# First edges of a graph layer: seven gather buffers of four chunks in place of three of eight, and a bfloat16 list of destinations

## The chip, the cores and the metric

The kernel runs on one core of one Trainium2 chip. The metric is the device time of one execution in microseconds; the time given is the median of several executions. A profile is one further execution, recorded by the hardware profiler: its span runs from the first to the last instruction, and its own time lies a little above the span.

## What is computed

One layer of a graph transformer over 6250 nodes of 256 features: a graph attention over 200000 edges sorted by destination, a linear attention over all nodes beside it, and then a mixture of four experts whose gate is itself a graph attention over 131072 edges.

```python
def reference(x, src, dst, W, a_src, a_dst, Wqkv, Wout, gamma, ...):
    xn = layernorm(x)
    # first edges
    z = einsum('ni,hid->nhd', xn, W)                  # 4 heads of 64
    es, ed = einsum('nhd,hd->nh', z, a_src), einsum('nhd,hd->nh', z, a_dst)
    e = leaky_relu(es[src] + ed[dst], 0.01)
    alpha = segment_softmax(e, dst)
    gnn = segment_sum(alpha * z[src], dst)
    x = x + gnn + linear_attention(xn, Wqkv, Wout, gamma)
    # second edges: a gate from a graph attention, top 2 of 4 experts
    return x + mixture_of_experts(layernorm(x), edge_index, ...)
```

## The kernel before

**Stages.** The kernel first normalizes the rows and projects them; for each node it stores a row of 264 floats, `z` with a one behind each head (260) and the four source terms, in the table `ztab` in DRAM. From the sorted edges it makes two lists on chip: `src_c`, for each edge the row of `ztab` to fetch, and `dl_c`, the destination's place within its tile of 128 nodes. Both are laid out with the edges of a chunk over the 128 partitions and one column per chunk; each tile of nodes has room for 33 chunks (28 for the last), 1612 chunks in all. Then comes the stage of the first edges, then that of the second edges with the experts.

**The first edges** (class `FirstEdges`, lines 762 to 854; its loop, 1018 to 1096). Chunks are taken in groups of `G1` = 8, 202 groups, the last of 4 chunks. For a group:

- `gather` (772, 774): one indirect DMA per chunk on POOL's queue fetches 128 rows of `ztab` into the group's tile `gt`, of 8 chunks. The pool `g1_g` has three such tiles.
- `sources` (786, with the helper at 208 to 210): VectorE subtracts the largest source term from the four terms of each gathered row (`L208`, into `src_d`), and ScalarE makes two exponentials of it (`src_f`).
- `load` (792): the destinations of the group's edges, spread to all partitions, are loaded on SP's queue as `br`; `one_hot_t` (807) compares them with the partition's number; `terms` (813) fetches the destination factors with matmuls against that one-hot matrix, and `terms_sum` (821) adds their three parts.
- `weights` (825, 827): each edge's weight, put into `dv`, a tile in PSUM that also holds the lane numbers.
- `weigh` (833): VectorE multiplies the gathered rows in place by the weights, four chunks at a time.
- `one_hot` (798): VectorE compares the lane numbers in `dv` with `dl_c`; the result `oh` is a float32 matrix per chunk.
- `add` (842): TensorE multiplies `oh` with the weighted rows, which sums them by destination; at a tile's end the sums are divided and stored (758 to 760, 849 to 851).

**What sets the order.** The loop writes the order out by hand. In turn g it begins with the gathers of group g+2 and the load of g+3, then does `weights`, `weigh` of chunks 0 to 3, `add` of those, `weigh` and `add` of chunks 4 to 7, with `terms`, `one_hot` and `sources` of group g+1 between and behind them. Between these stand small steps of the linear attention and the second norm (`mix_steps`; its row loads are line 978 and its joins with the sums 980 to 989), and the sort of the second edges. The framework tracks which instruction last used a piece of memory and adds the waits; it also moves instructions within an engine by its own estimate of their times, so the order on an engine is near that of the program but not always the same. A gather into a `gt` tile waits until the adds that read the tile's former content are done; POOL runs its queue in order, so what stands behind such a gather waits too.

**Ahead of and behind the stage.** A mask `before` (77) is made at the start and used only in `order_edges` (304, 305), a branch for edges that are not sorted. The lists are turned into columns by transposes and copied out of PSUM at 713. At the end of the stage the second norm writes its table `htab` (180, 181); the second edges gather from it at 1303, in groups of eight as well, 784 gathers; they write their one-hot matrix at 1324 and the messages at 1377. Their three short loads of the gate's norm are line 1268, the memsets of `first_of` are 1681 and 1683.

Of the kernel before, what the change touches and what calls it, by code (L numbers as in the profile page):

```python
# [9 lines left out]
F32 = mybir.dt.float32  # L10
BF16 = mybir.dt.bfloat16
I32 = mybir.dt.int32
U16 = mybir.dt.uint16
AF = mybir.ActivationFunctionType
OP = mybir.AluOpType
# [5 lines left out]
P = 128  # L21
# [4 lines left out]
EPS = 1e-5  # L26

G1 = 8
K1, K1L = 33, 28

ZW = 4 * 65
ZF = ZW + 4
# [29 lines left out]
def gps_layer(ctx: ExitStack, tc: tile.TileContext, a: dict, out: bass.AP):  # L62
# [9 lines left out]
    jp = cw.tile([P, P], I32, name="jp")  # L72
    G.iota(jp, pattern=[[1, P]], base=0, channel_multiplier=-1)
    ident = const.tile([P, P], F32, name="ident")
    V.tensor_scalar(ident, jp, 0.0, None, op0=OP.is_equal)
    before = const.tile([P, P], F32, name="before")
    V.tensor_scalar(before, jp, 0.0, None, op0=OP.is_gt)
    lane_i = cw.tile([P, P], I32, name="lane_i")
    G.iota(lane_i, pattern=[[1, P]], base=0, channel_multiplier=0)
    lane = const.tile([P, P], F32, name="lane")  # L80
# [119 lines left out]
    def source_factors(src_f, d, es, m2, slope):  # L200

        V.tensor_sub(d, es, m2[:, None, :].to_broadcast(list(es.shape)))  # L208
        S.activation(src_f[:, :, 0:4], d, AF.Exp, bias=shift_c)  # L209
        S.activation(src_f[:, :, 4:8], d, AF.Exp, scale=slope)  # L210

# [37 lines left out]
    S1 = len(chunk_tile)  # L249
    BS = (S1 + P - 1) // P  # L250
    src_c = ek.tile([P, BS * P], I32, name="src_c")
    dl_c = ek.tile([P, BS * P], F32, name="dl_c")
    over = ek.tile([1, 1], I32, name="over")
    start_k = ek.tile([P, 1], F32, name="start_k")
    first_t = ek.tile([P, B1], F32, name="first_t")
# [5 lines left out]
    def order_edges(w, bs, bd):  # L261

        C = (E1 + P - 1) // P
        room = kx.rearrange("p t d -> p (t d)")
        used = 0

        def take(n, dt, words):
            nonlocal used
            used += words
            assert used <= NT * D  # L270
            return room[:, used - words : used].bitcast(dt)[:, :n]

        o1, o2 = take(C, I32, C), take(C, I32, C)
        rec_ = take(2 * B1 * P, I32, 2 * B1 * P)
        R, rem = divmod(E1, C)
        pairs = dram.tile([B1 * P * P, 2], I32, name="pairs")
        src_i = o1
        dst_i = o2
        if rem:
            V.memset(src_i[96:P, rem:C], 0)  # L280
            V.memset(dst_i[96:P, rem:C], NT * P)
        for t_, d_ in ((src_i, a["src"]), (dst_i, a["dst"])):
            SP.dma_start(t_[:R], d_[0 : R * C].rearrange("(p c) -> p c", c=C))
            if rem:
                SP.dma_start(t_[R : R + 1, :rem], d_[R * C : E1].rearrange("(p c) -> p c", p=1))
        rec = rec_[:, : 2 * C].rearrange("p (c o) -> p c o", o=2)
        V.tensor_copy(rec[:, :, 0], src_i)
        V.tensor_copy(rec[:, :, 1], dst_i)
        addr = take(C, I32, C)
        V.tensor_single_scalar(addr, dst_i, 7, op=OP.arith_shift_right)  # L290
        tid = take(C, F32, C)
        V.tensor_scalar(tid, addr, float(NT), None, op0=OP.min)
        cnt = w.tile([P, NB], F32, name="cnt")
        hit = take(C, BF16, (C + 1) // 2)
        for b in range(NB):
            V.tensor_scalar(hit, tid, float(b), None, op0=OP.is_equal, op1=OP.add, accum_out=cnt[:, b : b + 1])
        off = w.tile([P, NB], F32, name="off")
        with tc.tile_pool(name="ord_p", bufs=1, space=PSUM) as ps:
            tot_p = ps.tile([NB, 1], F32, name="tot_p")
            T.matmul(tot_p, cnt, ones[:, 0:1], start=True, stop=True)  # L300
            tot = w.tile([NB, 1], F32, name="tot")
            V.tensor_copy(tot, tot_p)
            off_p = ps.tile([P, NB], F32, name="off_p")
            T.matmul(off_p, before, cnt, start=True, stop=False)
            T.matmul(off_p, tot[:, 0:1].to_broadcast([NB, P]), before[:NB, :NB], start=False, stop=True)
            V.tensor_copy(off, off_p)
        pos = o1.bitcast(F32)
        mask = take(C, U16, (C + 1) // 2)
        run = o2.bitcast(F32)
        for b in range(NB):  # L310
            V.tensor_scalar(mask, tid, float(b), None, op0=OP.is_equal)
            V.tensor_tensor_scan(run, mask, mask, off[:, b : b + 1], OP.add, OP.max)
            V.copy_predicated(pos, mask, run)
        V.tensor_scalar(addr, pos, 1.0, None, op0=OP.subtract)
        for c in range(C):
            i = G.indirect_dma_start(
                out=pairs[:, :],
                out_offset=bass.IndirectOffsetOnAxis(ap=addr[:, c : c + 1], axis=0),
                in_=rec[:, c, :],
                in_offset=None,  # L320
            )
            tc.declare_no_dep(i.ins, group="pairs", reason="each edge has a place of its own")
            tc.add_to_no_dep_group("pairs", i.ins)

        both = rec_.rearrange("p (b j o) -> p b j o", b=B1, o=2)
        V.tensor_copy(both[:, :, :, 0], bs)
        V.tensor_copy(both[:, :, :, 1], bd)
        full, r = divmod(E1, P * P)
        r, rest = divmod(r, P)
        if full:  # L330
            SP.dma_start(both[:, :full], pairs[0 : full * P * P].rearrange("(b r j) o -> r b j o", r=P, j=P))
        at = full * P * P
        if r:
            SP.dma_start(both[:r, full], pairs[at : at + r * P].rearrange("(r j) o -> r j o", j=P))
        if rest:
            at += r * P
            SP.dma_start(both[r : r + 1, full, :rest], pairs[at : at + rest].rearrange("(r j) o -> r j o", r=1))
        V.tensor_copy(bs, both[:, :, :, 0])
        V.tensor_copy(bd, both[:, :, :, 1])
# [422 lines left out]
    class FirstEdges:  # L762
# [6 lines left out]
            self.idx, self.dl, self.n, self.tiles = idx, dl, n, tiles  # L769

        def gather(self):
            self.gt = self.gp.tile([P, G1, ZF], F32, name="gt")
            for c in range(self.n):
                G.indirect_dma_start(  # L774
                    out=self.gt[:, c, :],
                    out_offset=None,
                    in_=ztab[:, :],
                    in_offset=bass.IndirectOffsetOnAxis(ap=self.idx[:, c : c + 1], axis=0),
                )

        def sources(self):

            n = self.n
            d = self.w.tile([P, G1, 4], F32, name="src_d", bufs=1)
            self.sf = self.w.tile([P, G1, 8], F32, name="src_f")
            source_factors(self.sf[:, :n], d[:, :n], self.gt[:, :n, ZW:], most_1, 0.01)

        def load(self, rows_):

# [31 lines left out]
            V.tensor_reduce(self.pw[:, :n], self.ed[:, :n].rearrange("p c (s f) -> p c f s", s=3), AX.X, OP.add)  # L821

        def weights(self):
            n, pw, gt = self.n, self.pw, self.gt
            V.tensor_mul(pw[:, :n], pw[:, :n], self.sf[:, :n])
            self.wp = self.dv[:, P : P + 4 * G1].rearrange("p (c h) -> p c h", h=4)
            V.tensor_max(self.wp[:, :n], pw[:, :n, 0:4], pw[:, :n, 4:8])

        def weigh(self, c0, c1):
            if c0 < self.n:  # L830
                c1 = min(c1, self.n)
                gz = self.gt[:, c0:c1, 0:ZW].rearrange("p c (h d) -> p c h d", h=4)
                V.tensor_mul(gz, gz, self.wp[:, c0:c1].unsqueeze(3).to_broadcast([P, c1 - c0, 4, 65]))  # L833

        def add(self, sums, s0, c0, c1):

            for c in range(c0, min(c1, self.n)):
                t = self.tiles[c]
                if t not in sums:
                    sums[t] = self.ps.tile([P, ZW], F32, name="ag")  # L840
                last = s0 + c + 1 == S1 or chunk_tile[s0 + c + 1] != t
                T.matmul(  # L842
                    sums[t], self.oh[:, c], self.gt[:, c, 0:ZW], start=(s0 + c == 0 or chunk_tile[s0 + c - 1] != t),
                    stop=last,
                )
                if last:
                    a3 = sums[t].rearrange("p (h d) -> p h d", h=4)
                    if t in joined:
                        z = self.w.tile([P, D], F32, name="z", bufs=1)
                        node_sums(self.w, a3[:, :, 0:64], a3[:, :, 64], z)  # L850
                        V.tensor_add(kx[: rows(t), t], kx[: rows(t), t], z[: rows(t)])
                    else:
                        node_sums(self.w, a3[:, :, 0:64], a3[:, :, 64], kx[:, t])
                    summed.add(t)
# [160 lines left out]

    n_hops = 2 * NT + 8 + 3 * NT + 10 + 6 * NT + 2 * NT + 26 + 5 * NT + 39

    with tc.tile_pool(name="g1_w", bufs=2) as w, tc.tile_pool(name="g1_g", bufs=3) as gp, tc.tile_pool(
        name="m_w", bufs=2
    ) as mxw, tc.tile_pool(name="m_k", bufs=1) as mxk, tc.tile_pool(name="g1_p", bufs=2, space=PSUM) as ps:  # L1020
        steps = mix_steps(mxw, mxk, ps)
# [76 lines left out]
    with tc.If(many != 0):  # L1098
# [7 lines left out]
        with tc.tile_pool(name="sl_k", bufs=1) as k, tc.tile_pool(name="sl_w", bufs=1) as w, tc.tile_pool(  # L1106
# [42 lines left out]
            with tc.For_i(0, NI, 1) as i:  # L1149
# [29 lines left out]
                grp.weights()  # L1179
                grp.weigh(0, 1)  # L1180
                ag = ps.tile([P, ZW], F32, name="ag")
                T.matmul(ag, grp.oh[:, 0], grp.gt[:, 0, 0:ZW], start=True, stop=True)
                a3 = ag.rearrange("p (h d) -> p h d", h=4)
                at = kx[:, ds(t, 1), :].rearrange("p a (h d) -> p (a h) d", h=4)
                V.tensor_add(at, at, a3[:, :, 0:64])
# [569 lines left out]
```

## Time and profile before

| | us |
|---|---|
| median of 3 runs | 3260.65 (3256.18 to 3268.05) |
| the profiled execution | 3258.8 |
| its span | 3257.0 |
| first gather of the first edges starts | 114.90 |
| last gather of the first edges ends | 2176.53 |
| first gather of the second edges starts | 2200.41 |
| last gather of the second edges ends | 3203.63 |

| engine | busy us | share of the span |
|---|---|---|
| DVE (VectorE) | 2439.4 | 75% |
| POOL (GpSimd) | 2344.4 | 72% |
| PE (TensorE) matmul | 2334.0 | 72% |
| PE weight load | 1699.4 | 52% |
| ACT (ScalarE) | 480.6 | 15% |

A line of a group of instructions reads: line of the kernel, engine, operation, written tile <- read tiles, number of instructions | busy time in us and mean ns of one | time for which the engine sat idle before them, and what ended most of that. In a timeline, a line reads: start and duration in us, engine, line, operation, tiles, and in brackets the engine's idle time before it and what ended it; "issue" is time in which the engine waited for nothing that the profile shows. Shares of busy time are means over stages that have different limits, so the stages are looked at one by one.

### The profile page before, as it was taken

The numbers are of one execution on the slowest core, as the hardware profiler recorded it, in microseconds if no ns is written. First come the engines' busy times: TensorE is split into PE (matmuls) and PEld (weight loads), VectorE is DVE, ScalarE is ACT, GpSimd is POOL, SyncE is SP. The second block draws the span as 40 slices with busy tenths as digits, with TensorE's granted clock in tenths as the row PEclk, the third lists the DMA queues.
The fourth block names the chain that finished last, engine by engine and source line by source line (L and its number), as shares of the span: only waits on it lengthen the run. The fifth ranks groups of instructions, "written<-read, shape, count | busy, mean of one in ns | idle before, by whom it ended". The sixth has DMA issues, their size and how long they took to land. (4 is left out here: it accounts for less than half of the span.)

```text
span 3257.0 us, 36396 instructions
## 1 busy us (share of the span) xinstructions
PE 2334.0 (72%) x10899; PEld 1699.4 (52%) x10900; DVE 2439.4 (75%) x6337; ACT 480.6 (15%) x1266; POOL 2344.4 (72%) x2436
## 2 busy tenths in 40 slices
PE   7677778865666574665665666658777877888888
PEld 5555666654455453554544545445455545555555
DVE  7587767788888887886886878667676766777775
ACT  3200111111111111111111111013111111111111
POOL 2577777777777777777777777757777777777772
PEclk9788888987888887787888878779998998999989
DMA  6544444445555555555555555534223223333321
GB/s 202 155 135 135 136 129 127 137 134 145 150 139 151 143 137 140 138 141 143 141 153 142 147 140 142 138 92 101 61 62 78 60 57 92 81 76 80 78 51 37
DMA packets 248273, 384.90 MB, mean 118 GB/s; under 512 B 73414, under 2 KB 156246, under 8 KB 248057
## 3 DMA queue, kind: packets, MB, share of 16 engines
q0 software_dynamic: 103296, 230.96, 28.9%
q1 hardware_dynamic: 142857, 150.87, 15.4%
q8 instruction: 91, 1.49, 0.2%
q14 instruction: 125, 1.02, 0.1%
q10 hardware_dynamic: 1904, 0.56, 0.1%
HBM read 345.44 MB, written 36.74 MB: 117 GB/s over the span
## 5 line engine op out<-in xcount | busy, mean ns | idle before, releaser
L774 POOL DMA_INDIRECT gt<-ztab,src_c x1612 | 1551.2, 962 | 528.1 <-issue 424.7
L842 PE MATMUL ag<-gt,oh 128*128 128x260 f32 x3224 | 980.1, 461 | 348.3 <-DVE gt L833 347.0
L842 PEld LDWEIGHTS ag<-gt,oh 128*128 128x128 f32 x3224 | 732.6, 234 | 516.0 <-DVE gt L833 375.9
L1303 POOL DMA_INDIRECT gt<-htab,src x784 | 764.6, 975 | 262.5 <-issue 210.0
L833 DVE TENSOR_TENSOR gt<-gt,dv 128x1040 f32<-128x1040 f32 x403 | 488.8, 1223 | 0.2 <-DVE src L409 0.2
L1424 PE MATMUL yo<-w,hT 128*128 128x256 f32 x1568 | 420.8, 411 | 15.8 <-DVE ys L1467 15.8
L1404 PE MATMUL hp<-xy,w 128*128 128x512 f32 (+1 forms) x832 | 407.2, 612 | 8.6 <-ACT hT L1409 4.5
L1424 PEld LDWEIGHTS yo<-w,hT 128*128 128x128 f32 x1568 | 303.5, 203 | 96.1 <-issue 26.3
L208 DVE TENSOR_TENSOR src_d<-gt,most 128x32 f32<-128x32 f32 x204 | 38.6, 189 | 355.6 <-DMA gt<-ztab,src_c 344.3
L868 PE MATMUL m<-wqkv,xy 128*128 128x256 f32 (+1 forms) x784 | 235.8, 436 | 88.8 <-DVE kmax L879 43.6
L798 DVE TENSOR_TENSOR oh<-dv,dl_c 128x1024 f32<-128x1024 f32 x202 | 243.9, 1207 | 0.0
L868 PEld LDWEIGHTS m<-wqkv,xy 128*128 128x128 f32 (+1 forms) x784 | 160.7, 215 | 125.1 <-DVE kmax L879 49.6
L1404 PEld LDWEIGHTS hp<-xy,w 128*128 128x128 f32 x832 | 159.9, 205 | 112.4 <-issue 98.3
L1409 ACT ACTIVATE hT<-hp,b 128x512 f32<-128x512 f32 (+1 forms) x208 | 132.8, 660 | 517.6 <-PE hp L1404 294.9
L209 ACT ACTIVATE src_f<-src_d,shift_c 128x32 f32<-128x32 f32 x202 | 64.9, 321 | 928.2 <-DVE src_d L208 836.3
L1361 DVE TENSOR_TENSOR pr<-dv,gt 128x64 f32<-128x64 f32 x98 | 21.9, 223 | 227.0 <-DMA gt<-htab,src 219.5
L1385 PE MATMUL ag<-mq,oh 128*128 128x120 bf16 x784 | 66.3, 236 | 150.4 <-DVE mq L1377 141.0
L813 PE MATMUL ed<-pw,ohT 128*128 128x24 bf16 x1612 | 72.1, 175 | 125.5 <-DVE ohT L807 111.1
L373 DVE MAX8 src<-dl 128x8 f32<-128x1024 f32 x128 | 156.0, 1219 | 0.4 <-issue 0.4
L1385 PEld LDWEIGHTS <-oh 128*128 128x128 bf16 x784 | 51.6, 107 | 198.5 <-DVE mq L1377 176.6
L375 DVE MATCH_REPLACE8 dl<-src,dl 128x1024 f32<-128x1024 f32 x127 | 153.4, 1208 | 0.0
L813 PEld LDWEIGHTS <-ohT 128*128 128x128 bf16 x1612 | 64.0, 98 | 165.4 <-DVE ohT L807 134.3
(350 smaller groups left out, 2695.0 us busy)
## 6 DMA issues: line engine op xcount, KB each, us to landing
br<-rows SPq DMA_DIRECT2D x299, 256.0 KB
gt<-ztab,src_c POOLq DMA_INDIRECT x1612
gt<-htab,src POOLq DMA_INDIRECT x784
early<-ys SPq DMA_DIRECT2D x24, 512.0 KB
ys<-early SPq DMA_DIRECT2D x24, 512.0 KB
ztab<-zt SPq DMA_DIRECT2D x48, 132.0 KB
row<-in_x_dram SPq DMA_DIRECT2D x48, 128.0 KB
out_dram<-ys SPq DMA_DIRECT2D x48, 128.0 KB
```

Of the source, the lines that this page charges most:

```text
L373: V.max(out=srtf[:, 8 * i : 8 * i + 8], in_=keyf)
L375: V.match_replace(out=keyf, in_to_replace=srtf[:, 8 * i : 8 * i + 8], in_values=keyf, imm_value=0.0)
L774: G.indirect_dma_start(out=self.gt[:, c, :], out_offset=None, in_=ztab[:, :], in_offset=bass.IndirectOffsetOnAxis(ap=self.idx[:, c : c + 1 ...
L798: V.tensor_tensor(self.oh[:, :n], self.dv[:, None, :P].to_broadcast([P, n, P]), self.dl[:, :, None].to_broadcast([P, n, P]), op=OP.is_equal,)
L813: T.matmul(self.ed[:, c, :], self.ohT[:, c * P : (c + 1) * P], pw3[:, ds(self.tiles[c], 1), :].rearrange("p a b -> p (a b)"), start=True, ...
L833: V.tensor_mul(gz, gz, self.wp[:, c0:c1].unsqueeze(3).to_broadcast([P, c1 - c0, 4, 65]))
L842: T.matmul(sums[t], self.oh[:, c], self.gt[:, c, 0:ZW], start=(s0 + c == 0 or chunk_tile[s0 + c - 1] != t), stop=last,)
L868: T.matmul(out_, xy[:, t, j, :n], wqkv[:, j, c0 : c0 + D], start=(j == 0), stop=(j == 1))
L1303: G.indirect_dma_start(out=self.gt[:, c, : tab.shape[1]], out_offset=None, in_=tab[:, :], in_offset=bass.IndirectOffsetOnAxis(ap=self.idx[ ...
L1404: T.matmul(hp[:, :m], wts[e][0][:, c, j * P : (j + 1) * P], xy[:, t0 : t0 + nt, c] if m == nt * P else xy[:, t0, c, :m], start=(c == 0), s ...
L1409: S.activation(h[:, :m], hp[:, :m], AF.Gelu, bias=b1[:, e, j : j + 1])
L1424: T.matmul(yo[:n], hT[j][:, o : o + n], wts[e][1][:, j, :], start=(j == 0 and e < EARLY), stop=(j == 3))
```

## The change

The tile of a group's gathered rows is split: `gather` takes a new tile of `GH` = 4 chunks from the pool at chunks 0 and 4, and the pool has seven such tiles, room for 28 chunks in place of 24. The functions that read `gt` take the tile and the chunk within it. `sources` makes its subtraction once per tile of four, and one pair of exponentials for the group as before (the helper `source_factors` is cut in two for it). The list `dl_c` is held as bfloat16, in half the memory; it holds whole numbers within a tile. The mask `before` is now made in the branch that uses it.

```diff
@@
 G1 = 8
+GH = 4
@@
-    before = const.tile([P, P], F32, name="before")
-    V.tensor_scalar(before, jp, 0.0, None, op0=OP.is_gt)
@@
         V.tensor_sub(d, es, m2[:, None, :].to_broadcast(list(es.shape)))
+        factors_of(src_f, d, slope)
+
+    def factors_of(src_f, d, slope):
         S.activation(src_f[:, :, 0:4], d, AF.Exp, bias=shift_c)
         S.activation(src_f[:, :, 4:8], d, AF.Exp, scale=slope)
@@
-    dl_c = ek.tile([P, BS * P], F32, name="dl_c")
+    dl_c = ek.tile([P, BS * P], BF16, name="dl_c")
@@ in order_edges
+        jp_ = w.tile([P, P], I32, name="jp_")
+        G.iota(jp_, pattern=[[1, P]], base=0, channel_multiplier=-1)
+        before = w.tile([P, P], F32, name="before")
+        V.tensor_scalar(before, jp_, 0.0, None, op0=OP.is_gt)
@@ FirstEdges.gather
-            self.gt = self.gp.tile([P, G1, ZF], F32, name="gt")
+            self.gt = []
             for c in range(self.n):
+                if c % GH == 0:
+                    self.gt.append(self.gp.tile([P, GH, ZF], F32, name="gt"))
                 G.indirect_dma_start(
-                    out=self.gt[:, c, :],
+                    out=self.gt[-1][:, c % GH, :],
@@ FirstEdges.sources
-            source_factors(self.sf[:, :n], d[:, :n], self.gt[:, :n, ZW:], most_1, 0.01)
+            for c0 in range(0, n, GH):
+                c1 = min(c0 + GH, n)
+                V.tensor_sub(
+                    d[:, c0:c1], self.gt[c0 // GH][:, : c1 - c0, ZW:], most_1[:, None, :].to_broadcast([P, c1 - c0, 4])
+                )
+            factors_of(self.sf[:, :n], d[:, :n], 0.01)
@@ FirstEdges.weigh
-                gz = self.gt[:, c0:c1, 0:ZW].rearrange("p c (h d) -> p c h d", h=4)
+                gz = self.gt[c0 // GH][:, : c1 - c0, 0:ZW].rearrange("p c (h d) -> p c h d", h=4)
@@ FirstEdges.add
-                    sums[t], self.oh[:, c], self.gt[:, c, 0:ZW], start=(s0 + c == 0 or chunk_tile[s0 + c - 1] != t),
+                    sums[t], self.oh[:, c], self.gt[c // GH][:, c % GH, 0:ZW], start=(s0 + c == 0 or chunk_tile[s0 + c - 1] != t),
@@
-    with tc.tile_pool(name="g1_w", bufs=2) as w, tc.tile_pool(name="g1_g", bufs=3) as gp, tc.tile_pool(
+    with tc.tile_pool(name="g1_w", bufs=2) as w, tc.tile_pool(name="g1_g", bufs=7) as gp, tc.tile_pool(
```

More of the change, by code (lines that the diff above doesn't have):

```diff
@@ L823, in weights @@
         def weights(self):
-            n, pw, gt = self.n, self.pw, self.gt
+            n, pw = self.n, self.pw
             V.tensor_mul(pw[:, :n], pw[:, :n], self.sf[:, :n])
@@ L1181, in gps_layer @@
                 ag = ps.tile([P, ZW], F32, name="ag")
-                T.matmul(ag, grp.oh[:, 0], grp.gt[:, 0, 0:ZW], start=True, stop=True)
+                T.matmul(ag, grp.oh[:, 0], grp.gt[0][:, 0, 0:ZW], start=True, stop=True)
                 a3 = ag.rearrange("p (h d) -> p h d", h=4)
```

## The prediction

> **What bounds the kernel now.** I read the page first, groups of instructions then waits. `L774` is the gather of the first edges, 1612 on POOL's queue.
>
> ```profile
> L774 POOL DMA_INDIRECT gt<-ztab,src_c x1612 | 1551.2, 962 | 528.1 <-issue 424.7
> L208 DVE TENSOR_TENSOR src_d<-gt,most 128x32 f32<-128x32 f32 x204 | 38.6, 189 | 355.6 <-DMA gt<-ztab,src_c 344.3
> L798 DVE TENSOR_TENSOR oh<-dv,dl_c 128x1024 f32<-128x1024 f32 x202 | 243.9, 1207 | 0.0
> ```
>
> POOL's 528.1 us of idle are mostly "issue": time in which it waited for nothing shown. VectorE waits 344.3 us at `L208` for gathers to land. So POOL feeds this stage, VectorE follows it. The table by stretches gives the sizes.
>
> ```profile
> 115.00:2176.00 2061.00, 1368.62 (x6387) 1076.43 (x6388) 1609.89 (x3883) 267.09 (x771) 1550.57 (x1612) 0.82 0.51 140
> 2201.00:3204.00 1003.00, 826.34 (x3890) 520.02 (x3890) 717.00 (x2002) 160.24 (x314) 763.99 (x784) 0.92 0.32 73
> ```
>
> The columns are start:end, length, busy time of PE, its weight loads, DVE, ACT, POOL, then clock, DMA share and GB/s. The first line is the stage that the diff touches; DVE is 78% busy in it (1609.9 of 2061.0). The timeline of POOL alone shows what the gathers do in detail.
>
> ```profile
> 436.61 0.95 POOL L774 DMA_INDIRECT gt<-ztab,src_c  x1 [0.30 <-issue]
> 437.86 0.95 POOL L774 DMA_INDIRECT gt<-ztab,src_c  x1 [0.30 <-issue]
> 442.11 0.94 POOL L774 DMA_INDIRECT gt<-ztab,src_c  x1 [3.31 <-PE ag L842]
> 443.36 0.95 POOL L774 DMA_INDIRECT gt<-ztab,src_c  x1 [0.30 <-issue]
> ```
>
> A gather takes 0.95 and is followed by 0.30 of issue, so one starts every 1.25 us whoever else works. 1612 x 1.25 = 2015 us of the 2061.6 from 114.90 to 2176.53. The rest is 20 us of stalls like the one at 442.11 (below), and about 26 us by which some gathers last longer than 0.95 (their mean is 962 ns, not 946). The stall at 442.11 is the first chunk of a group: its buffer is free only when the adds (`L842`) of the group three back have read it.
>
> **Part 1: the buffers.** Going through every gather of the stage in that view, all but 16 start within 0.4 us of the previous one's end. One is the stage's first (17.65 us, on the work before the stage). The other 15 idle 1.45, 3.31, 1.78, 1.32, 3.29, 1.20, 0.79, 2.05, 2.15, 1.49, 1.32, 2.00, 0.56, 0.43 and 1.02 us: 24.16 in all, less the 15 x 0.30 of issue = **19.7 us**. All 15 are first chunks of a group. This is all that more room can give back, 0.6% of the run; the page's 37.4 us for POOL on PE `L842` counts the 0.30 of every harmless first chunk too.
>
> Is it given back? Before, chunk 0 of group g+2 waits for the last add of group g-1. After, tile 0 of g+2 takes the place of the second tile of g-2, a whole group older; tile 1, four gathers or 5.0 us later, takes that of the first tile of g-1, whose adds stand ahead of those of the second. So the late add is no longer what chunk 0 waits for, and chunk 4 needs an earlier one 5.0 us later: over 5 us of new slack against a longest stall of 3.0 (3.31 - 0.30), or 4.2 for the two in a row at 429.11 and 442.11. It would not suffice if the lag added up. It doesn't: at `L208`, VectorE's lag behind the end of its group's last gather is about 2.2 us when it waits for the landing; it rises to 10.7 at worst (group 140) and is back at 2.3 five groups later; in groups 187 to 197 it is about 2.2 in all but one. I take all 19.7.
>
> POOL gets a second waiting instruction per group, chunk 4. Behind it on POOL's queue stand all later gathers, and VectorE's `L208` waits for those. A wait that is already met costs nothing: first chunks without a stall show 0.301 us of gap, other chunks 0.300. 202 x 0.001 = 0.2 us, taken as 0.
>
> **Part 2: source factors in two subtractions.** Per group one `L208` of 128x32 becomes two of 128x16, back to back in the built order. The last group is of four chunks and shows the small form:
>
> ```profile
> 2180.55 0.17 DVE L208 TENSOR_TENSOR src_d<-gt,most 128x16 f32<-128x16 f32 x1
> ```
>
> On VectorE, 201 x (2 x 0.17 - 0.19) = 30 us more busy; in the stream, where the next operation starts 0.11 us after an `L208` start, some 22 us. It lies beside the gathers: VectorE idles 344.3 us at this very line, and where it waits, the first half is done before the last gather lands. If that cover were gone it would be 22 to 30 us of path. Taken as 0.
>
> These instructions have both inputs in SBUF, and here a rule speaks against the change. The Trainium skill (SBUF — State Buffer, "Who interferes with whom") says that such a VectorE instruction takes the read interface shared with GpSimd, so that a GpSimd instruction that reads SBUF waits for it in full. A gather reads its index list `src_c` there. By the rule, 201 more subtractions of 0.17 us are up to 34 us on the bounding queue. The row:
>
> ```profile
> 1017.78 0.95 POOL L774 DMA_INDIRECT gt<-ztab,src_c  x1 [0.30 <-issue]
> 1017.88 0.19 DVE L208 TENSOR_TENSOR src_d<-gt,most 128x32 f32<-128x32 f32 x1
> ```
>
> The subtraction lies within the gather, which keeps its 0.95. Over the stage, 188 gathers overlap an `L208` and average 0.962 us; the other 1424 average 0.964. Long ones do interfere: the 88 gathers beside the 256-wide operations of `L981` to `L988` average 1.089 against 0.957, one of them (1225.90) 2.55. So the price is between 0 (the short row) and 34 us (the rule in full); I take the row of the same instruction, 0, and keep 34 for a rival.
>
> **Part 3: the bfloat16 list and the rest.** `L798` reads `dl_c` as one of its inputs, the other is `dv` in PSUM, and writes float32. No row has this mix. Near it is `L1324`, the same shape with bfloat16 output at 1214 ns, and `L1377`, with bfloat16 in and out at 1151 ns for 960 elements: no faster per element. Bounds: 0, or 1% of 243.9 us = 2 either way, on an engine with cover; 0. The list's copies (`L713`, 0.68 us for 512) keep their count and width. The mask `before` leaves the start (one 128x128 `L77` on VectorE) for a branch that this execution didn't take: at most 0.3 us, under the loads of the start.
>
> Memory moves, so the built order moves some instructions. Two row loads (`L978`, SP) that stood in the start now go right ahead of the first `br` loads: about 0.7 us on SP's queue, where the first one-hot waits, but the first `L208` waits 7.17 us for gathers anyhow. The three small `L1268` loads go ahead of the last table stores, some 2 us of SP's queue in the 6 us between 2188.9 and 2195.0 in which SP has nothing to issue. Four small memsets go ahead of the end of the stage, under 0.3 us in a chain of waits. The next stage starts 23.9 us after the last gather, behind the last sums, the last norm and the table's stores (it is put down to a memset, `L1683`; the built gather waits for the stores and an earlier row). Nothing of this chain is shortened, and 784 gathers after it are paced by POOL alone (1003 us). So the whole span moves up by what POOL saves.
>
> **Sum.** 3258.8 (the profiled execution: span 3257.0 and 1.8 around it) - 19.7 + 0 = 3239.1. The median shown, 3260.65, is 1.85 above that execution; on its level the forecast is **3241 us**, -0.6%. The three runs before spread over 12 us, and long gathers shift by how they meet VectorE's work, so +-8: 3233 to 3249.
>
> **Rivals.**
> - *VectorE takes over as bound* (half or none of it arrives). Stalls come where VectorE or PE is late: with POOL no longer held, lag could pile up until chunk 4 stalls, or be handed to the end of the stage. For it: 78% busy, plus 1%. Against: lag back at 2.2 after each burst, and waits for landings up to group 200 (6.65 us). Half kept: 3260.65 - 9.8 = 3251; none: 3261.
> - *The added subtractions block gathers*: one mechanism at POOL, 201 x 0.17 = 34 us by the rule, less 19.7: **3275**, slower than before. It decides from 0.10 us per group on (19.7 / 202). For it: the rule, and the long operations that do delay gathers. Against: 188 overlaps at no cost.
> - *The wider room is used for nothing*, since POOL never runs ahead: true of all but 15 of 202 groups, and already in the sum.
>
> **How the numbers follow.** About 0.5% (16.3 us) is what a measurement of this kernel can tell from no change: below 3244.3 faster, above 3276.9 slower. Chances: forecast 0.66, VectorE bound 0.18, blocked gathers 0.16. Some 0.56 of the 0.66 lies below 3244.3; half of the last case, with mishaps not thought of, lies above 3276.9, so faster 0.56, same 0.36, slower 0.08. The range 3232 to 3263 holds the forecast with its margin and the first rival; above it, most of the last rival is left out.
>
> **What would show it.** Right: no gap over 0.4 us between gathers after the first, the stage's gathers done in about 2042 us instead of 2061.6, gathers still at 962 ns on the mean, twice the `src_d` rows at about 0.17, `oh` at 1207, and the 23.9 us and the second stage as they were. Wrong: stalls at chunk 4 (first rival), gathers at 980 ns or more (second), or a start of the second stage further behind the last gather.

## The result, and the profile after

| | median us | ratio to the kernel before, 95% interval |
|---|---|---|
| before | 3266.5 (7 runs, 3256.18 to 3268.66) | |
| after | 3246.7 (7 runs, 3236.85 to 3251.84) | 0.9943 [0.9927, 0.9958] |
| after, in another series (before 3266.2 there) | 3243.6 (4 runs) | 0.9924 [0.9905, 0.9942] |

The changed kernel is faster by 0.57%, and by 0.76% in the second series. The first eight experiments fell into series in which the kernel before itself took 3953.8 us (e1 to e4) or 4008.6 us (e5 to e8), at a mean granted TensorE clock of 0.78 to 0.79 instead of 0.85 to 0.86 and with engines standing still for up to 26 us at a time (in e1) on something that the profile calls only "remote"; each ratio is therefore to the kernel before in the same series.

The groups of instructions of the kernel after (the gather, the subtraction and the one-hot comparison are now lines 782, 796 and 811):

```profile
L782 POOL DMA_INDIRECT gt<-ztab,src_c x1612 | 1550.2, 962 | 508.7 <-issue 378.0
L796 DVE TENSOR_TENSOR src_d<-gt,most 128x16 f32<-128x16 f32 x403 | 62.5, 169 | 301.4 <-DMA gt<-ztab,src_c 300.6
L811 DVE TENSOR_TENSOR oh<-dv,dl_c 128x1024 f32<-128x1024 f32 x202 | 244.0, 1208 | 0.0
```

The gathers are neither fewer nor shorter: 1550.2 us busy and 962 ns each. What went is idle time before them, 528.1 to 508.7 us. The subtraction is there twice as often. The table by stretches of the kernel after:

```profile
114.00:2155.00 2041.00, 1390.64 (x6391) 1091.28 (x6392) 1628.81 (x4083) 265.82 (x771) 1550.20 (x1612) 0.81 0.53 141
2181.00:3193.00 1012.00, 820.88 (x3891) 515.49 (x3891) 717.95 (x2002) 159.16 (x313) 772.46 (x784) 0.93 0.34 72
```

The first stage is 20 us shorter with the same POOL work and 19 us more VectorE work. The second is 9 us longer; its busy POOL time has gone from 763.99 to 772.46, so its gathers last longer. Whether that is the change's doing is a question for the experiments. POOL's timeline, where the kernel before stalled at 442.11:

```profile
435.84 0.94 POOL L782 DMA_INDIRECT gt<-ztab,src_c  x1 [0.30 <-DVE gt L846]
437.09 0.94 POOL L782 DMA_INDIRECT gt<-ztab,src_c  x1 [0.30 <-issue]
438.33 0.94 POOL L782 DMA_INDIRECT gt<-ztab,src_c  x1 [0.30 <-issue]
```

The line at 437.09 is the same gather, the first chunk of group 32. It has its 0.30 us of issue and nothing more. It starts 5.0 us earlier: 3.0 from this stall, 1.15 from the one at 429.11, 0.8 from an earlier start of the stage. In the whole stage no gather after the first has more than 0.31 us ahead of it.

Cut into pieces, with two executions of each kernel (the second of each is e9 and e10 below), and two partial versions in the same manner:

| us | before | after | six of four, e11 | split alone, e12 |
|---|---|---|---|---|
| start to first gather | 114.9, 112.8 | 114.1, 117.4 | 116.2 | 114.6 |
| first to last gather of the first edges | 2061.6, 2062.0 | 2040.9, 2040.7 | 2042.1 | 2047.5 |
| of it stalls (number) | 19.6 (15), 19.1 (17) | 0, 0 | 0 | 6.3 (9) |
| to the first gather of the second edges | 23.9, 24.3 | 26.5, 25.3 | 24.6 | 25.5 |
| first to last gather of the second edges | 1003.2, 1010.1 | 1011.1, 1005.1 | 1005.3 | 1005.5 |
| rest | 53.4, 52.3 | 52.0, 53.3 | 53.4 | 53.4 |
| span | 3257.0, 3261.6 | 3244.6, 3241.8 | 3241.5 | 3246.6 |

On the means of two, the first stage gives 21.0 us and the other pieces take back 4.9 (start 1.9, boundary 1.8, second stage 1.4, rest -0.2), so the span is 16.1 us shorter. The stage's gain is steady to 1 us; the pieces outside it vary by up to 7 us between executions of one and the same kernel.

### The profile page after: what moved, and what is told of

The parts are those of the page before. It is cut to its first block, busy times and chain, and to the rows that moved or that the text cites. A ratio compares the mean times of both kernels' runs of the same rounds, so it can differ in the third digit from the quotient of the medians.

```text
span 3244.6 us, 36789 instructions
## 1 busy us (share of the span) xinstructions
PE 2347.0 (72%) x10899; PEld 1707.0 (53%) x10900; DVE 2457.9 (76%) x6537; ACT 479.2 (15%) x1266; POOL 2351.4 (72%) x2436
## 3 DMA queue, kind: packets, MB, share of 16 engines
q1 hardware_dynamic: 142857, 150.87, 16.1%
## 5 line engine op out<-in xcount | busy, mean ns | idle before, releaser
L782 POOL DMA_INDIRECT gt<-ztab,src_c x1612 | 1550.2, 962 | 508.7 <-issue 378.0
L855 PE MATMUL ag<-gt,oh 128*128 128x260 f32 x3224 | 1010.0, 473 | 341.6 <-DVE gt L846 338.8
L855 PEld LDWEIGHTS ag<-gt,oh 128*128 128x128 f32 x3224 | 750.2, 240 | 519.3 <-DVE gt L846 374.1
L1316 POOL DMA_INDIRECT gt<-htab,src x784 | 772.5, 985 | 265.1 <-issue 213.0
L796 DVE TENSOR_TENSOR src_d<-gt,most 128x16 f32<-128x16 f32 x403 | 62.5, 169 | 301.4 <-DMA gt<-ztab,src_c 300.6
L811 DVE TENSOR_TENSOR oh<-dv,dl_c 128x1024 f32<-128x1024 f32 x202 | 244.0, 1208 | 0.0
L381 DVE MATCH_REPLACE8 dl<-src,dl 128x1024 f32<-128x1024 f32 x127 | 153.4, 1208 | 0.0
```

The costliest lines, as they stand in the source:

```text
L381: V.match_replace(out=keyf, in_to_replace=srtf[:, 8 * i : 8 * i + 8], in_values=keyf, imm_value=0.0)
L782: G.indirect_dma_start(out=self.gt[-1][:, c % GH, :], out_offset=None, in_=ztab[:, :], in_offset=bass.IndirectOffsetOnAxis(ap=self.idx[:, ...
L811: V.tensor_tensor(self.oh[:, :n], self.dv[:, None, :P].to_broadcast([P, n, P]), self.dl[:, :, None].to_broadcast([P, n, P]), op=OP.is_equal,)
L855: T.matmul(sums[t], self.oh[:, c], self.gt[c // GH][:, c % GH, 0:ZW], start=(s0 + c == 0 or chunk_tile[s0 + c - 1] != t), stop=last,)
L1316: G.indirect_dma_start(out=self.gt[:, c, : tab.shape[1]], out_offset=None, in_=tab[:, :], in_offset=bass.IndirectOffsetOnAxis(ap=self.idx[ ...
```

## The experiments

**The theories.** Mine: the fifteen stalls at first chunks go because a group's buffer is handed back in halves, and nothing else in the change counts. Rivals: the extra four chunks of room do it (which the bfloat16 list pays for); the bfloat16 list or the moved mask does it by moving instructions; the split subtraction has a part, for good or ill; two SBUF inputs on VectorE hold up gathers, in the first stage or in the second.

**Taking the change apart, in the first series: e1 to e4.** e1 is the changed kernel once more.

> The changed kernel once more, for a second profile. Theory (POOL's stalls are what was won): the gathers of the first edges take 2041 us +-3 from first start to last end, none waits over 0.4 us after the first, time 0.5 to 0.7% below the kernel before. The second edges' gathers took 1011 us in the first profile of the changed kernel and 1003 before; if that is only how gathers happen to meet VectorE's message products (L1390), it falls anywhere between 1000 and 1012 here. Rival: the change itself lengthens the second stage, and it is 1011 again, within 2.

e2 has six buffers of four chunks, the room of before:

```diff
-... tc.tile_pool(name="g1_g", bufs=7) as gp, ...
+... tc.tile_pool(name="g1_g", bufs=6) as gp, ...
```

> Six buffers of four: the room of before (24 chunks) with release by four. Theory (the finer release does it: chunk 0 waits for the adds of the first half of the group before, chunk 4 for those of the second half 5.0 us later): stalls of 0 to 3 us in all, time within 0.1% of the changed kernel, so 16 to 20 us below before. Rival (the extra room of four chunks does it): stalls stay at 12 to 20 us and the time stays within 8 us of before.

e3 is the kernel before with the list and the mask of the change:

```diff
-    before = const.tile([P, P], F32, name="before")
-    V.tensor_scalar(before, jp, 0.0, None, op0=OP.is_gt)
@@
-    dl_c = ek.tile([P, BS * P], F32, name="dl_c")
+    dl_c = ek.tile([P, BS * P], BF16, name="dl_c")
@@ in order_edges: the mask is made there, as in the change (left out)
```

> Three buffers of eight as before, with the bfloat16 list and the moved mask alone. Theory: nothing, stalls at 15 to 24 us, L798 at 1207 ns +-5, time within 5 us of before. Rival (memory placement or the narrower list speeds the stage): 8 to 20 us below before.

e4 is the kernel before with two subtractions a group, and still three buffers of eight:

```diff
-            source_factors(self.sf[:, :n], d[:, :n], self.gt[:, :n, ZW:], most_1, 0.01)
+            for c0 in range(0, n, 4):
+                c1 = min(c0 + 4, n)
+                V.tensor_sub(d[:, c0:c1], self.gt[:, c0:c1, ZW:], most_1[:, None, :].to_broadcast([P, c1 - c0, 4]))
+            S.activation(self.sf[:, :n, 0:4], d[:, :n], AF.Exp, bias=shift_c)
+            S.activation(self.sf[:, :n, 4:8], d[:, :n], AF.Exp, scale=0.01)
```

> Three buffers of eight as before, with the subtraction of the source terms in two instructions alone. Theory (short subtractions cost POOL nothing): gathers at 962 ns +-5, stalls at 15 to 24 us, time within 5 us of before. Rival (each further instruction with two inputs in SBUF holds up a gather in full): gathers at about 983 ns, time up by 20 to 34 us.

| | median us | ratio to before (3953.8) | stalls in the first stage, us (number) |
|---|---|---|---|
| e1, the change | 3936.3 | 0.9944 [0.9912, 0.9975] | 400 (151) |
| e2, six of four | 3932.8 | 0.9953 [0.9925, 0.9981] | 404 (151) |
| e3, list and mask alone | 3953.9 | 0.9991 [0.9972, 1.0009] | 407 (124) |
| e4, split alone | 3960.8 | 1.0009 [0.9979, 1.0038] | 436 (130) |

The ratios came as the theory has them: versions with the halves gain, with 28 chunks of room or 24; the list and the mask bring nothing, and neither does the split alone. Its gathers took 960 ns, where the rival had 983. The stalls came otherwise: some 400 us in all four. In these profiles engines wait for "remote", which the profiles of before and after don't show. One line from e1's timeline:

```profile
912.74 0.37 ACT L971 COPY qT<-m 128x256 f32<-128x256 f32 x1 [19.13 <-remote]
```

What it copies had been written at 897.12; PE and VectorE wait behind it meanwhile, and then POOL for its buffers. In e1, 101 of the 151 stalls are at chunk 4 of a group, the form that the prediction gave for its first rival, since there VectorE really is late. Among 400 us of these, the fifteen stalls can't be counted, so the fate of the stalls stayed open after these four runs, and with it by what way the gain of e1 and e2 comes about in that series.

**The same with the float32 list: e5.** Six buffers of four as in e2, on the kernel before, with the list and the mask as they were.

> Six buffers of four with the float32 list and the mask where they were: the split of the buffers alone. Theory: the same as six of four with the bfloat16 list, stalls 0 to 3 us, 14 to 22 us below before. Rival (the list is part of the gain): less than 10 us below before.

3980.1 us against 4008.6 of before, ratio 0.994 [0.991, 0.997]: the whole gain without the bfloat16 list. The 0 to 3 us of stalls that I expected did not come: there are 171, with 435 us.

**Do two SBUF inputs hold up gathers? e6 and e7.** To six buffers of four I added one 128x512 addition a group whose result is used by nothing. In e6 both inputs are in SBUF; in e7, the control, one is in PSUM.

```diff
# e6
+            V.tensor_add(xtra, lane[:, None, :].to_broadcast([P, 4, P]), ident[:, None, :].to_broadcast([P, 4, P]))
# e7
+            V.tensor_add(xtra, self.dv[:, None, :P].to_broadcast([P, 4, P]), ident[:, None, :].to_broadcast([P, 4, P]))
```

> Six of four, with one more VectorE addition of 128x512 float32 per group behind the source terms (202 in all; about 0.7 us each), both inputs in SBUF; its result is not used. Theory (such an instruction delays a gather only if the gather comes to its read of SBUF while it runs, so the price grows with the square of its length): mean delay about 0.7 x 0.35 / 1.25 = 0.2 us each, 40 us in all, gathers at about 985 ns. By the rule in full (each delays a gather by its whole length): 141 us and 1050 ns. If two inputs in SBUF don't matter: the time and the gathers of the control with one input in PSUM.

> The control: the same added instruction, with one input in SBUF and the other (the lane numbers) in PSUM. Theory: gathers at 962 ns +-6; VectorE has 141 us more work under 300 us of waits for landings, so a few stalls of POOL come back, 0 to 15 us above six of four. Rival (any VectorE work of this length slows the gathers): gathers as with both inputs in SBUF.

The gather's group in e6:

```profile
L782 POOL DMA_INDIRECT gt<-ztab,src_c x1612 | 1572.4, 975 | 987.1 <-issue 402.8
```

and in e7:

```profile
L782 POOL DMA_INDIRECT gt<-ztab,src_c x1612 | 1550.0, 962 | 990.7 <-issue 410.8
```

The busy times can be compared, since 1550 us is also what the profiles before and after show. Two SBUF inputs cost the gathers 22.4 us, 0.11 us for each of the 202 additions; one costs nothing. The excess lies where the additions are: the 219 gathers beside one averaged 1064 ns in e6, the 215 in e7 973. So the interference is real, but far from the additions' whole length (141 us by the rule in full), and about half of the 40 us of my estimate. On the whole time the two can't be told apart: 4037.4 us (ratio 1.0076 [1.0049, 1.0103]) and 4031.4 (1.0089 [1.0050, 1.0128]). Both are slower than e5, by 57 and 51 us, where I had expected 0 to 15 for the control. I put that down to VectorE's added time, since VectorE is late in that series anyhow; this is not shown.

**The second stage's gathers: e8.** In the second stage the message product `mq` (line 1390) reads two SBUF inputs for 1.15 us. e8 is the changed kernel with a copy of one of them, `ohq`, into spare PSUM, from where `mq` reads it. It adds one copy a group.

```diff
+                V.tensor_copy(self.ohp, self.ohq)
@@ (the lines that give ohp its place in PSUM are left out)
-                    self.ohq[:, :, :, None].to_broadcast([P, G2, W2, 3 * HW]),
+                    self.ohp[:, :, :, None].to_broadcast([P, G2, W2, 3 * HW]),
```

> The changed kernel, and in the second edges a copy of the column selector ohq in PSUM, from which the message product mq reads it, so that this instruction (1.15 us, 98 of them) has one input in SBUF instead of two. Theory (in the second stage the gathers' time over 0.945 us, 22 us before and 30 after, is mostly this product in the way): gathers of the second edges from 973 to 983 ns down to about 955, the second stage shorter by 12 to 20 us than the changed kernel, time about 3230. Rival (gathers vary for another reason): the second stage stays at 1003 to 1011 us, time as the changed kernel or up to 5 us more for the 98 added copies.

The group in e7 and then in e8:

```profile
L1318 POOL DMA_INDIRECT gt<-htab,src x784 | 776.1, 990 | 520.3 <-issue 227.9 <-DVE dv L1380 199.8 <-SPq L1113 30.2
```

```profile
L1316 POOL DMA_INDIRECT gt<-htab,src x784 | 745.6, 951 | 614.5 <-DVE dv L1381 269.5
```

The mechanism is there: the gathers fell to 951 ns, from 989 to 999 ns in e1 to e7. It is those beside the product that became shorter: 148 of them averaged 1155 ns in e7, 129 averaged 958 in e8, and the others 952 and 950. But POOL's idle time before the gathers is 614.5 us, where e7 of the same series has 520.3. The profile puts 269.5 us of it down to VectorE (`L1381`), in e7 199.8 us to the same step (`L1380` there); VectorE has the copy more to do. The second stage is longer, 1327.5 us against 1266.3 in e7, not the 12 to 20 us shorter that I expected. The whole is 1.0122 [1.0094, 1.0149], slower. Whether the copy would pay where VectorE isn't late was not tried.

**A second profile of the kernel before: e9.**

> The kernel before, unchanged, for a second profile of it. If the earlier profile is typical: gathers of the first stage 962 ns, fifteen to a few more stalls at first chunks of groups, second stage's gathers 975 ns and some 1003 us from the first to the last of them. If the second stage's gathers vary by 10 ns from run to run with nothing changed, the 7.8 us by which the changed kernel's second stage was longer is no effect of the change; if they come at 975 ns again, it may be one.

One execution of 3263.4 us, beside another of 3265.4. The gathers of the second edges in the first profile of before, and in e9:

```profile
L1303 POOL DMA_INDIRECT gt<-htab,src x784 | 764.6, 975 | 262.5 <-issue 210.0
```

```profile
L1303 POOL DMA_INDIRECT gt<-htab,src x784 | 771.5, 984 | 263.0 <-issue 214.6
```

The unchanged kernel shows 984 ns and 1010.1 us here, where its first profile had 975 ns and 1003.2. So the second stage varies by 7 us with nothing changed. The stalls are back in the same places, 13 of the 17 at groups that stalled in the first profile as well, with 19.1 us instead of 19.6.

**The parts again, where the kernel before takes 3266 us: e10 to e12.** The same kernels as e1, e5 and e4.

> The changed kernel, unchanged. Theory (the room in half groups takes the fifteen stalls away, and nothing else counts): ratio 0.994, first stage's gathers from first to last in some 2041 us with no stall. Rival on the second stage (its 7.8 us more belong to the change): its gathers again at 985 ns and in some 1011 us, against 975 ns and 1003 us of the kernel before; if the 7.8 us are chance, anything from 1003 to 1011 us.

> Six buffers of four chunks (the same 24 chunks of room as before), float32 list, mask where it was. Theory (handing the room back in halves is what counts): ratio 0.994, no or nearly no stall in the first stage. Rival (the 25th to 28th chunk of room, which the bfloat16 list pays for, is what counts): ratio 0.998 to 1.000 and several of the fifteen stalls left.

> The kernel before with the subtraction of a group in two instructions, still three buffers of eight chunks. Theory: the subtraction isn't what stalls, so the stalls stay, some 15 of them and 20 us; two subtractions for one cost nothing; ratio 1.000. Rival (the earlier result of the first half of a group's numbers lets the scales, the scaling and the freeing of buffers run ahead): ratio 0.996 or less and fewer stalls. Rival (VectorE takes 23 us more and delays the chain): ratio 1.004.

| | median us | ratio to before (3266.2) |
|---|---|---|
| e10, the change | 3243.6 | 0.9924 [0.9905, 0.9942] |
| e11, six of four, float32 list | 3240.8 | 0.9919 [0.9891, 0.9948] |
| e12, split alone | 3250.5 | 0.9947 [0.9930, 0.9964] |

e10 against e11: the list, the mask and the four chunks of extra room bring nothing that can be measured. In e10 the gathers of the second edges are the opposite of e9's surprise:

```profile
L1316 POOL DMA_INDIRECT gt<-htab,src x784 | 766.5, 978 | 264.0 <-issue 213.0
```

The changed kernel now has 978 ns and 1005.1 us, less than e9 has. The longer second stage of the first profile after is chance.

e12 is where my theory of "nothing else counts" fell, and the rival with a ratio of 0.996 or less and fewer stalls came. With three buffers of eight, as before, the split alone takes 14.1 us from the stage and leaves 6.3 of 19.6 us of stalls. The same kernel brought nothing as e4 (1.0009 [0.9979, 1.0038]), in the series with some 400 us of stalls. So the share of the split depends on what else holds the engines up; what follows holds where the kernel before takes 3266 us.

## How the split takes stalls away

A stall of the kernel before, followed through its timeline (gathers and other work left out):

```profile
1664.14 0.19 DVE L208 TENSOR_TENSOR src_d<-gt,most 128x32 f32<-128x32 f32 x1 [8.62 <-DMA gt<-ztab,src_c]
...
1665.02 1.22 DVE L833 TENSOR_TENSOR gt<-gt,dv 128x1040 f32<-128x1040 f32 x1
...
1666.49 1.20 DVE L833 TENSOR_TENSOR gt<-gt,dv 128x1040 f32<-128x1040 f32 x1
...
1669.03 3.90 PE L842 MATMUL ag<-gt,oh 128*128 128x260 f32 x14
...
1673.20 0.96 POOL L774 DMA_INDIRECT gt<-ztab,src_c  x1 [1.32 <-PE ag L842]
```

VectorE stands 8.62 us at the subtraction of group 150, until that group's eighth chunk has landed. Behind it in VectorE's order stand the two scalings of group 149, behind those PE's adds, and behind those POOL's first gather of group 152, which takes 149's buffer. The sum is close: group 150's last gather ended at 1661.88, the subtraction came 2.26 us later, the buffer's release 9.06 us after that, 11.32 in all. POOL has eight gathers for cover, 10.01 us from 1661.88 to 1671.89, and 0.30 of issue: 11.32 - 10.31 = 1.01 us of stall. Such a wait of over 4 us lies 8 to 12 us ahead of 12 of the 15 stalls. The stall is a small difference of two large times, so a little off the chain takes much of it. The same group in e12:

```profile
1647.79 0.17 DVE L788 TENSOR_TENSOR src_d<-gt,most 128x16 f32<-128x16 f32 x1 [3.42 <-DMA gt<-ztab,src_c]
...
1651.49 0.17 DVE L788 TENSOR_TENSOR src_d<-gt,most 128x16 f32<-128x16 f32 x1 [3.53 <-DMA gt<-ztab,src_c]
...
1652.21 1.22 DVE L837 TENSOR_TENSOR gt<-gt,dv 128x1040 f32<-128x1040 f32 x1
...
1653.69 1.21 DVE L837 TENSOR_TENSOR gt<-gt,dv 128x1040 f32<-128x1040 f32 x1
...
1658.25 1.92 PE L846 MATMUL ag<-gt,oh 128*128 128x260 f32 x8
...
1660.44 0.95 POOL L774 DMA_INDIRECT gt<-ztab,src_c  x1 [0.90 <-PE ag L846]
```

The first half waits for the group's fourth chunk, the second for the eighth. The last gather ended at 1649.54, so the second half runs 1.95 us behind it instead of 2.26, and the release follows 8.95 us later: a stall of 0.60. Over the stage, where VectorE waited for an eighth chunk, the median from the end of its gather to the subtraction is 2.27 and 2.30 us in the two profiles of before, 2.05 in e12, and 2.03 and 2.05 in those of after. Taking 0.25 us off each of the fifteen stalls gives 3.6 of the 13.3 us. The trace doesn't say why the second half starts sooner.

Most of the rest goes with the order of VectorE's instructions, which the framework plans and which one more instruction has changed. In the kernel before, the subtraction of a group stands ahead of both scalings of the group before it in 24 of 200 groups, and behind them in 176. All fifteen stalls come two groups after one of the 24 (in e9 14 of 17): there a wait of the subtraction holds up the scalings too. In e12 the second half stands ahead in 17 groups: ten of the 24 have moved behind, three others ahead. Six of the fifteen stalls belong to the ten, 7.5 us in all, and none of the six is left. One is the longest, the 3.31 us at 442.11 that the prediction shows. Group 30's subtraction and group 29's scalings in the kernel before:

```profile
430.68 0.19 DVE L208 TENSOR_TENSOR src_d<-gt,most 128x32 f32<-128x32 f32 x1 [4.57 <-DMA gt<-ztab,src_c]
...
433.62 1.23 DVE L833 TENSOR_TENSOR gt<-gt,dv 128x1040 f32<-128x1040 f32 x1
...
434.85 1.20 DVE L833 TENSOR_TENSOR gt<-gt,dv 128x1040 f32<-128x1040 f32 x1
```

The same in e12, with the first gather of group 32:

```profile
426.70 1.23 DVE L837 TENSOR_TENSOR gt<-gt,dv 128x1040 f32<-128x1040 f32 x1
...
428.81 1.23 DVE L837 TENSOR_TENSOR gt<-gt,dv 128x1040 f32<-128x1040 f32 x1
...
432.20 0.25 DVE L788 TENSOR_TENSOR src_d<-gt,most 128x16 f32<-128x16 f32 x2
...
439.41 0.95 POOL L774 DMA_INDIRECT gt<-ztab,src_c  x1 [0.30 <-issue]
```

The other nine stalls went from 12.1 to 3.8 us, and four groups that had not stalled before have 2.5 us in e12. Shorter waits are not the reason: the waits of a group at the subtraction come to 5 us or more in 18 groups of before and in 18 of e12. No run changes the order and leaves the subtraction whole, so the share of the order is read from the rows, not shown by a run of its own. e11 and the changed kernel have the order of e12, e3 that of before.

What the halves of the buffers add to the split: the last 6.3 us of stalls are gone, in e11 and in the change alike, and the stage is 5.5 us (e11) and 6.6 to 6.9 us (the change) shorter than in e12. Halves without the split can't be had, since the subtraction reads both tiles; whether they would have taken all 19.7 us by themselves is therefore not shown. Four buffers of eight, the room without the halves, were not tried.

## Why the prediction was right, point by point

- **The bound.** Right. The gathers pace the stage in before, after and e9 to e12: 961 to 963 ns each with 0.30 us of issue, and without stalls 2041 to 2043 us from the first to the last.
- **The stalls, 19.7 us.** Right in size and place. They are gone in both profiles after, and the stage is 20.7 and 21.3 us shorter. A second wait per group, at chunk 4, costs nothing: its mean gap is 0.305 us, and so is that of the others.
- **The cause of the stalls.** Half right. Late adds do hold the buffer, but behind them stands VectorE, at the subtraction of the next group. I read that wait of 344.3 us only as a sign that VectorE follows POOL, and not where in VectorE's order it stands.
- **The split taken as 0.** This step was wrong, though the sum didn't suffer: by itself the split gives 14.1 us of the stage (e12); by the rows, more than half of the stalls that it removes goes with the changed order of instructions, which I had not thought of. Since both parts take away the same stalls, they don't add up to 35. Its price was as worked out: VectorE's subtractions take 62.5 us instead of 38.6, 24 more against the 22 to 30 that I gave, and they are hidden.
- **Two SBUF inputs, taken as 0 here.** Right: 962 ns before and after. e6 shows why the rule that the prediction cites couldn't be dropped for longer instructions: 0.11 us per addition of 512 elements. My averages over single gathers were made of rounded times and are 1 to 2 ns too high: 960.5 ns beside a subtraction and 962.5 for the others, 1088 beside the wide operations and 955 for the rest. The comparison stands.
- **The bfloat16 list and the mask, 0.** Right: `oh` at 1208 ns against 1207; e3 at 0.9991, and e10 equal to e11.
- **The other stages as they were.** True within their own variation. The second stage is at 1003 to 1010 us before and 1005 to 1011 after. The boundary is 1.8 us longer on the means; six of four has 24.6 and the split alone 25.5, so I can't name a part of the change as its cause, and the load that was moved was not tried alone.
- **The number.** 3239.1 for the profiled execution, where 3246.7 and 3243.9 were seen. The difference is the start, the boundary and the second stage. As a ratio, 19.7 of 3260.65 is -0.60%, against -0.57% and -0.76%. The median of 3246.7 is 5.7 us above the forecast of 3241; that of before, over seven runs, is about as much above the 3260.65 of the first three. So the two medians lie 19.8 us apart, and that this meets the 19.7 so closely is luck: by the profiles the stage gave 21.0 us and the other pieces took back 4.9.
- **The rivals.** VectorE as the bound did not come: no stall at chunk 4. In the series of e1 it did, 101 times, and the change still kept its 0.6%. Blocked gathers did not come.

## What to carry to other kernels

When an engine waits for a buffer, follow the release back through the engines that work in order. Here it led to a wait of VectorE for another group's landing, with the releasing work queued behind it. Where a framework plans the order, compare the order of the rows before and after, too: one more instruction moved ten of 24 such places. Two parts of a change that remove the same stalls have to be tried one by one, since neither the sum nor the result of the whole tells their shares. And before a stage that the change doesn't touch is explained, profile the unchanged kernel twice.

## What the runs showed of the hardware that I had not expected

- A subtraction that waited for a group's eighth landing started 2.27 to 2.30 us (median) after the end of that gather on POOL when it was whole, and 2.03 to 2.06 us as a second half. A first half that waited for the fourth landing took 2.3 to 2.7 us (16 to 18 groups a profile), so the number of landings is not what makes the difference; the cause is open.
- The same program's gathers in the second stage took 975 or 984 ns on the mean, and 985 or 978 in the changed kernel, in different executions: 7 us of time.
- A VectorE addition of 512 elements with two SBUF inputs lengthened gathers by 0.11 us a piece; the subtractions of 16 elements did not at all; and with one input of the 1.15 us product moved to PSUM, the gathers beside that product averaged 958 ns, where e7 has 1155.
